# Sparse-graph layer and routed experts on one core: columns of A by way of memory, and by transfers inside the chip

## The chip, the core and the metric

The kernel runs on one core of a Trainium2 chip. Its metric is the device time of one execution in microseconds (us). Three runs of the kernel before gave 504.09, 504.42 and 505.32 us, a median of 504.42. All arithmetic of the parts discussed here is in float32, apart from the one-hot matrices in bf16.

## The reference, cut to what matters

```
x: [2048, 256]; src, dst: 67584 edges, sorted by dst; edge_weight: [67584]
xn  = layernorm(x)
x   = x + segment_sum(edge_weight[:, None] * xn[dst], src, 2048) + node_vec1
xt  = layernorm(x)                              # 2048 tokens of 256
top 2 of 8 experts by softmax(xt @ Wr + br)
x   = x + sum over the two of weight * (gelu(LN(xt) @ W1[e] + b1[e]) @ W2[e] + b2[e])
```

The first part is a sparse 2048 x 2048 matrix A (about 33 entries a column) times xn. The second part is a mixture of experts.

## The kernel before

**Building A densely.** The kernel turns A into dense blocks. A "column block" cb (0 to 15) is the 128 columns of A that meet the 128 rows of xn in block cb; a "half block" n (0 to 31) is 64 of these columns, so cb = n // 2 and h = n % 2 is its half. The loop over n (L463) goes once round for each half block:

- `make_hots(n + 1)` (L299 to L327): VectorE builds the one-hot matrices `hl` (rows within a block, L306) and `eq` (L311) for the next half block and multiplies two thirds of the weights in (L318); GpSimd multiplies the last third (`third`, L325).
- `make_cols(n)` (L329 to L350): TensorE multiplies the one-hots of each group of edges (L343) into the PSUM tile `pa` (3 buffers, two of them used per half block); ScalarE copies each to the SBUF tile `ar` (L346; 3 buffers). In `ar` a partition is a pair of a column and a block of rows, which is not what the later product needs: there a partition must be a column alone. So the rows are turned round by way of memory: SyncE stores `ar` to the DRAM tile `ad` (L347, 512 KB, in rows of 512 bytes), and after the second half reads the whole of it back as the SBUF tile `ac` (L350, 1 MB; partition = column, 8 KB each).
- `dense(cbs, b)` (L352 to L359): TensorE multiplies a group of `ac` tiles with `xn_sb` into the PSUM tile `py1` (2 buffers) for two row blocks b and b + 1, and `add` (L361) puts the result onto `acc` on VectorE, one round later.

**The order.** It is written out by hand: each engine executes its own instructions in the order in which the program names them, SyncE its transfers too. Groups of column blocks are 0-2, 3-5, 6-8, 9-11 and 12-15 (`CS`); each group has 8 calls of `dense`. `todo` holds all 40 calls. From n = 8 on (L500) each round adds 3.5 to a budget, and a call of `dense` costs as much as its group has column blocks (L502 to L504). In the last round (n = 31) all calls of the first four groups that are left are made; the 8 calls of group 12-15 come after the loop (L1077 onward), with the routing and the experts behind them. Between the loop and these stands a branch that all engines take part in (L569).

**Buffers of ac.** Groups take the pools `cols_1` and `cols_0` in turn (`pool_of`, L178), each with 4 buffers. The first tile of a group goes to the one buffer that the group two before it left free; the second tile (blocks 7, 10, 13) goes where that earlier group's first tile was, and so has to wait for the last call of `dense` on that group. The tile `ac` is allocated at h = 1, just ahead of its read (L349).

**After the loop.** SyncE goes on with the weights of the first experts (L932 to L935), the routing runs on VectorE, ScalarE and TensorE, and then TensorE works through the experts' slots (L1013, L1027) until the end.

Of the kernel before, what the change touches and what calls it, by code (L numbers as in the profile page):

```python
# [9 lines left out]
F32 = mybir.dt.float32  # L10
# [11 lines left out]
P = 128  # L22
# [4 lines left out]
def kernel(  # L27
# [30 lines left out]
    nc = tc.nc  # L58
# [3 lines left out]
    NB = N // P  # L62
# [3 lines left out]
    GC = 2  # L66
# [3 lines left out]
    GB = P // GC  # L70
    GH = GB // 2
    QP = P // RK
# [15 lines left out]
    dram = ctx.enter_context(tc.tile_pool(name="dram", bufs=1, space=DRAM))  # L88
# [89 lines left out]
    pool_of = {cb: (cols_1, cols_0)[g % 2] for g, cbs in enumerate(groups) for cb in cbs}  # L178
# [150 lines left out]
    def make_cols(n, hl, hr):  # L329


        cb, h = n // 2, n % 2
        if h == 0:
            ads[cb] = dram.tile([P, NB, P], F32, name="ad", bufs=4)
        ad_v = ads[cb].rearrange("(m j) b r -> (j b) m r", m=GB // QP)
        ar = rowsp.tile([P, GH // QP, P], F32, name="ar")
        for m0 in range(0, GH // QP, 4):
            pa = ps_a.tile([P, 4, P], F32, name="pa")
            for m in range(4):
                for i in range(3):  # L340
                    for j in range(QP):
                        g = (m0 + m) * QP + j
                        nc.tensor.matmul(pa[j * RK:(j + 1) * RK, m, :], hr[:, i, g, :],  # L343
                                         hl[:, g, :], start=(i == 0), stop=(i == 2),
                                         tile_position=(0, j * RK))
            nc.scalar.copy(ar[:, m0:m0 + 4, :], pa)  # L346
        nc.sync.dma_start(ad_v[:, h * GH // QP:(h + 1) * GH // QP, :], ar)  # L347
        if h == 1:
            acs[cb] = pool_of[cb].tile([P, NB, P], F32, name="ac")  # L349
            nc.sync.dma_start(acs[cb], ads[cb])  # L350

    def dense(cbs, b):  # L352

# [14 lines left out]
                                           acc[:, b + i, :D], op0=OP.add, op1=OP.add)  # L368
        nc.vector.tensor_add(acc[:, b:b + 2, D:], acc[:, b:b + 2, D:], pa[:, :, D:DX])

    ads, acs = {}, {}
    ET = mybir.EngineType
    ALL = {ET.DVE, ET.Pool, ET.PE, ET.Activation, ET.SP}
    with tc.manual_schedule(engines=ALL):
# [88 lines left out]
        for n in range(NH):  # L463
# [3 lines left out]
            m = n % 4  # L467
# [26 lines left out]
            for p in late:  # L494
                add(*p)
            late = []
            make_cols(n, *hots.pop(n))


            if n >= 8:  # L500
                budget += 3.5
            while len(todo) > NB // 2 and (budget >= len(todo[0][0]) or n == NH - 1):  # L502
                cbs, b = todo.pop(0)
# [17 lines left out]
            if n == 1:  # L521
# [5 lines left out]
                for rows in (b1_rows, g_rows, be_rows, nv_rows):  # L527
                    m = rows.shape[0]
# [40 lines left out]
    with tc.If(n_used < E):  # L569
# [11 lines left out]
        with tc.tile_pool(name="any", bufs=2) as anyp, tc.tile_pool(  # L581
            name="ps_any", bufs=2, space=PSUM
# [594 lines left out]
    with tc.manual_schedule(engines=ALL - {ET.Pool}):  # L1177
        for q in range(4):
            r = slice(q * N // 4, (q + 1) * N // 4)
# [33 lines left out]
```

## Time and profile before

| What | Value |
|---|---|
| Runs: median (lowest to highest) | 504.42 us (504.09 to 505.32) |
| The profiled execution: its own time | 508.05 us |
| Its span, first to last instruction | 506.3 us, mean granted TensorE clock 0.945 |
| TensorE busy with matmuls | 459.8 us (91%) |
| VectorE, ScalarE, GpSimd busy | 273.1, 183.8, 192.7 us |
| First and last store to `ad` (L347) begun | 31.0 and 192.5 us |
| Read of `ac` (L350): 16, issue to landing | 4.9 to 6.2 us, median 5.9 |
| Store to `ad` (L347): 32, issue to landing | 4.4 to 9.9 us, median 8.7 |
| Dense products of the last group begin (L357) | 209.4 us |

Times inside the execution are counted from the start of the span. A share of busy time is an average: for one stage the busy time of each engine in that stretch is to be read. PE is TensorE, DVE VectorE, ACT ScalarE, POOL GpSimd, SP SyncE; a q behind the name is the engine's queue of transfers, waits and branches. A line such as "ACT ar L346 <- DMA ad<-ar: 5.3, 3, 2.6" says that ScalarE stood 5.3 us in all, 3 times, 2.6 us at the longest, before line 346, until the transfer named had landed.

### The profile page before, as it was taken

What the parts mean: (1) busy time and instruction counts of PE and PEld (TensorE: products, weight loads), DVE (VectorE), ACT (ScalarE), POOL (GpSimd) and SP (SyncE); (2) the same over time, 40 slices, a digit from 0 to 9 for tenths busy, and PEclk for the clock granted to TensorE, in tenths of its full rate; (3) what the DMA queues carried; (4) which work ended last, traced back from release to release, by engine and by line L of the source; (5) the groups of instructions that cost most, each with busy time, mean ns of one, the idle gap of its engine ahead of it and who ended that gap; (6) DMA issues with size and microseconds to landing.
All of it is one profiled execution on the core that took longest, in us unless ns stands there. A gap on an engine that the chain in (4) does not pass through costs nothing.

```text
span 506.3 us, 12113 instructions
## 1 busy us (share of the span) xinstructions
PE 459.8 (91%) x4996; PEld 394.4 (78%) x4996; DVE 273.1 (54%) x621; ACT 183.8 (36%) x422; POOL 192.7 (38%) x158
## 2 busy tenths in 40 slices
PE   4876599898979999899999899999999999999993
PEld 3775478687758878788888788888888888888882
DVE  7999999999969971317837232323232312212111
ACT  2478524144214210028483323332243433333320
POOL 3477655544533330000142444443452444322231
PEclk9575679899979999999999999999999999999998
DMA  6128678796777667953513997997999677226420
GB/s 214 53 76 246 203 223 269 230 236 186 203 216 221 210 178 239 344 189 105 179 54 84 303 333 214 361 356 210 334 360 309 169 210 210 36 40 204 140 92 31
DMA packets 84356, 102.15 MB, mean 202 GB/s; under 512 B 8240, under 2 KB 74656, under 8 KB 82176
## 3 DMA queue, kind: packets, MB, share of 16 engines
q1 hardware_dynamic: 74832, 86.26, 53.5%
q0 software_dynamic: 7984, 13.91, 11.9%
q10 hardware_dynamic: 1472, 1.06, 0.7%
q8 instruction: 44, 0.72, 0.6%
q14 instruction: 24, 0.20, 0.1%
HBM read 75.18 MB, written 28.14 MB: 204 GB/s over the span
## 4 chain that ended last, share of the span: by engine, by line
PE 35%; DMA 13%; issue 3%; DVE 1%; SPq 0%; ACT 0%; POOL 0%; POOLq 0%; DVEq 0%
PE py L1027 16%; PE ph L1013 15%; DMA xs<-xr_d,to_i 8%; DMA y_d<-ys,to_i 2%; DMA out<-y_d 2%; PE px L978 1%; PE px L834 1%; PE py L357 1%; DMA so_far<-out,to_i 1%; DMA out<-ys,to_i 0%; SPq L1180 0%; POOL out L1048 0%; POOLq L1209 0%; ACT L1015 0%; DVE pick L957 0%
## 5 line engine op out<-in xcount | busy, mean ns | idle before, releaser
L357 PE MATMUL py<-xn_sb,ac 128*128 128x264 f32 x512 | 126.3, 404 | 1.8 <-DVEq L569 1.4
L1013 PE MATMUL ph<-xeT,w 128*128 128x256 f32 (+1 forms) x576 | 121.3, 368 | 2.4 <-PEq L1167 1.7
L1027 PE MATMUL py<-w,hT 128*128 128x256 f32 x544 | 121.0, 379 | 0.0
L1013 PEld LDWEIGHTS ph<-xeT,w 128*128 128x128 f32 x576 | 104.4, 190 | 16.5 <-issue 3.0
L357 PEld LDWEIGHTS py<-xn_sb,ac 128*128 128x128 f32 x512 | 98.5, 197 | 21.7 <-issue 2.2
L1027 PEld LDWEIGHTS py<-w,hT 128*128 128x128 f32 x544 | 101.9, 190 | 12.9
L1015 ACT ACTIVATE hT<-ph,ec 128x256 f32<-128x256 f32 (+1 forms) x144 | 66.2, 462 | 117.6 <-PE ph L1013 60.8
L1035 POOL DMA_INDIRECT y_d<-ys,to_i x30 | 48.5, 1616 | 119.3 <-DVE ys L1030 88.5
L318 POOL TENSOR_TENSOR hr<-eq,w 128x1024 bf16<-128x1024 bf16 x32 | 61.2, 1912 | 81.6 <-DVE hr L318 66.1
L343 PE MATMUL pa<-hl,hr 128*32 128x128 bf16 x3072 | 58.4, 237 | 21.6 <-POOL hr L318 10.8
L343 PEld LDWEIGHTS <-hr 128*32 128x32 bf16 x3072 | 50.0, 106 | 32.6 <-issue 14.0
L306 DVE TENSOR_TENSOR hl<-k,iota_t 128x4096 bf16<-128x4096 bf16 x32 | 72.9, 2278 | 0.0
L987 DVE TENSOR_SCALAR xeT<-px,ec 128x256 f32<-128x256 f32 (+1 forms) x38 | 18.4, 526 | 79.8 <-PE px L978 79.0
L939 POOL DMA_INDIRECT xs<-xr_d,to_i x39 | 40.5, 1038 | 54.2 <-DVE z L702 41.9
L346 ACT COPY ar<-pa 128x512 f32<-128x512 f32 x64 | 36.5, 584 | 59.8 <-PE pa L343 53.6
L1030 DVE SCALAR_TENSOR_TENSOR ys<-py,wt,b2w 128x256 f32<-128x256 f32 x34 | 16.4, 484 | 72.7 <-PE py L1027 61.3
L364 DVE TENSOR_TENSOR acc<-acc,py 128x528 f32<-128x528 f32 x32 | 22.3, 701 | 35.3 <-PE py L357 35.3
L318 DVE TENSOR_TENSOR hr<-eq,w 128x2048 bf16<-128x2048 bf16 x32 | 39.1, 1223 | 0.6
L1002 ACT ACTIVATE b2w<-b,wt 128x256 f32<-128x256 f32 x36 | 16.3, 500 | 34.0 <-DVE wt L1000 32.4
L311 DVE TENSOR_TENSOR eq<-k,iota_t 128x1024 bf16<-128x1024 bf16 x32 | 21.8, 680 | 0.0
L670 ACT ACTIVATE sq<-acc,less_m 128x256 f32<-128x256 f32 x16 | 8.0, 499 | 32.6 <-DVE acc L364 32.6
L296 ACT CAST w<-r 128x256 bf16<-128x256 f32 x16 | 6.5, 405 | 25.0 <-DVE r L295 25.0
(196 smaller groups left out, 303.0 us busy)
## 6 DMA issues: line engine op xcount, KB each, us to landing
w<-in_L_ffn_W SPq DMA_DIRECT2D x40, 1024.0 KB, 9.2
ad<-ar SPq DMA_DIRECT2D x32, 512.0 KB, 8.7
ac<-ad SPq DMA_DIRECT2D x16, 1024.0 KB, 5.9
b<-in_L_ffn_b SPq DMA_DIRECT2D x20, 128.0 KB, 9.8
out<-y_d SPq DMA_DIRECT2D x4, 512.0 KB, 6.3
xr_d<-rec SPq DMA_DIRECT2D x1, 1300.0 KB
y_d<-acc SPq DMA_DIRECT2D x1, 1280.0 KB, 5.1
acc<-in_x SPq DMA_DIRECT2D x2, 512.0 KB, 7.6
```

Source lines behind the costliest of these rows:

```text
L306: nc.vector.tensor_tensor(hl.rearrange("p g (n t) -> p g n t", t=2), two(k2[:, 0], g, P), pair(P), OP.is_equal)
L311: nc.vector.tensor_tensor(eq.rearrange("p g (n t) -> p g n t", t=2), two(k2[:, 1], g, RK), pair(RK), OP.is_equal)
L318: return engine.tensor_tensor(hr[:, i0:i1].rearrange("p i g (n t) -> p (i g) n t", t=2), eq[:, None, :, :].to_broadcast([P, i1 - i0, GH, RK]),
L343: nc.tensor.matmul(pa[j * RK:(j + 1) * RK, m, :], hr[:, i, g, :], hl[:, g, :], start=(i == 0), stop=(i == 2), tile_position=(0, j * RK))
L346: nc.scalar.copy(ar[:, m0:m0 + 4, :], pa)
L357: nc.tensor.matmul(pa[:, i, :DX], acs[c][:, b + i, :], xn_sb[:, c, :], start=(c == cbs[0]), stop=(c == cbs[-1]))
L364: nc.vector.tensor_add(acc[:, b:b + 2, :], acc[:, b:b + 2, :], pa[:, :, :DX])
L939: nc.gpsimd.indirect_dma_start(out=(sets[s.set][0] if into is None else into)[:, t, :], out_offset=None, in_=(xr_d if rows is None else ro ...
L1013: nc.tensor.matmul(ph, w1[:, k, c * P:(c + 1) * P], xeT[:, k, :], start=(k == 0), stop=(k == KD - 1))
L1015: nc.scalar.activation(hT[:, c, :s.n * P], ph, AF.Gelu, bias=ec[:, c:c + 1], scale=1.0)
L1027: nc.tensor.matmul(py, hT[:, c, t * P:(t + 1) * P], w2[:, c, :], start=(c == 0), stop=(c == KH - 1))
L1035: st = nc.gpsimd.indirect_dma_start(out=y_d[:, :], out_offset=bass.IndirectOffsetOnAxis(ap=tos[s.to][:, t:t + 1], axis=0), in_=ys, in_offs ...
```

## The change

The rows are turned round without memory: each half block's `ar` goes to `ac` in eight transfers from SBUF to SBUF. Transfer m takes one 128 x 128 slice of `ar` (64 KB: 128 partitions of 512 bytes) to 8 partitions of `ac` (8 KB each). Four are begun after each of the two copies; SyncE begins m = 0 to 4 and ScalarE m = 5 to 7. The tile `ac` is allocated at h = 0, one half block earlier than before. The budget for dense products starts at n = 7, not 8.

```diff
         cb, h = n // 2, n % 2
         if h == 0:
-            ads[cb] = dram.tile([P, NB, P], F32, name="ad", bufs=4)
-        ad_v = ads[cb].rearrange("(m j) b r -> (j b) m r", m=GB // QP)
+            acs[cb] = pool_of[cb].tile([P, NB, P], F32, name="ac")
         ar = rowsp.tile([P, GH // QP, P], F32, name="ar")
         for m0 in range(0, GH // QP, 4):
             pa = ps_a.tile([P, 4, P], F32, name="pa")
...
             nc.scalar.copy(ar[:, m0:m0 + 4, :], pa)
-        nc.sync.dma_start(ad_v[:, h * GH // QP:(h + 1) * GH // QP, :], ar)
-        if h == 1:
-            acs[cb] = pool_of[cb].tile([P, NB, P], F32, name="ac")
-            nc.sync.dma_start(acs[cb], ads[cb])
+            for m in range(m0, m0 + 4):
+
+                c = (h * GH // QP + m) * QP * GC
+                queue = nc.sync if m < 5 else nc.scalar
+                queue.dma_start(acs[cb][c:c + QP * GC], ar[:, m, :])
...
-    ads, acs = {}, {}
+    acs = {}
...
-            if n >= 8:
+            if n >= 7:
                 budget += 3.5
```

Here P = 128, NB = 16, GH = 32, QP = 4, GC = 2, so GH // QP = 8 slices and QP * GC = 8 partitions.

## The prediction

> **What bounds the kernel now.** I read the busy time by stretch first, since the averages of the page mix stages. Columns: length, then busy time of TensorE, its weight loads, VectorE, ScalarE, GpSimd, then granted clock, DMA share, GB/s. The stretches are the loop before and after dense products begin, its tail, and the last group.
>
> ```profile
> 31.00:70.00 39.00, 27.85 (x820) 23.45 (x820) 38.65 (x46) 26.07 (x66) 27.92 (x20) 0.69 0.70 208
> 70.00:190.00 120.00, 111.52 (x2439) 90.58 (x2437) 108.44 (x139) 37.84 (x88) 52.55 (x33) 0.96 0.74 215
> 190.00:209.00 19.00, 17.63 (x160) 14.85 (x160) 4.23 (x6) 1.17 (x2) 0.88 (x4) 1.00 0.84 274
> 209.00:240.00 31.00, 30.43 (x145) 25.85 (x146) 13.55 (x36) 14.23 (x41) 0.00 (x0) 1.00 0.56 188
> ```
>
> To 70 us VectorE is full (38.65 of 39). From 70 to 190 TensorE (111.5 of 120) and VectorE (108.4) are nearly level. Behind 190 TensorE alone sets the end. The DMA engines are three quarters busy throughout.
>
> The waits, second, inside that loop (60 to 192 us; SyncE 30 to 200):
>
> ```profile
> PE pa L343 <- issue: 6.6, 4, 3.1
> PE py L357 <- DMA ac<-ad: 0.4, 1, 0.4
> ACT ar L346 <- DMA ad<-ar: 5.3, 3, 2.6
> DVE acc L364 <- PE py L357: 6.1, 3, 4.2
> SPq L350 <- DMA ad<-ar: 102.9, 19, 9.3
> SPq L350 <- PE py L357: 2.5, 2, 2.3
> ```
>
> SyncE stands 102.9 us for its own stores before it may read back, and stores of later half blocks queue behind. So `ar` comes free late, ScalarE's copy waits 5.3 us, TensorE has holes of 6.6 us and VectorE then waits (4.2 us once). That is all the way through memory costs on the path: about 7 us. The arrival of `ac` itself costs 0.4 us.
>
> Third, the tail in order of time (start, length, what):
>
> ```profile
> 190.42 1.41 PE L343 MATMUL pa<-hl,hr 128*32 128x128 bf16 x88 [1.78 <-POOLq L569]
> 191.76 16.29 PE L357 MATMUL py<-xn_sb,ac 128*128 128x264 f32 x72
> ...
> 198.34 0.33 SPq L350 DMA_DIRECT2D ac<-ad  x1
> ...
> 209.45 0.91 PE L357 MATMUL py<-xn_sb,ac 128*128 128x264 f32 x3 [1.40 <-DVEq L569]
> ```
>
> From 191.76 to 208.0 TensorE works off the dense calls that are left: 72 matmuls, 12 a call, so 6 calls of 2.7 us. Then comes the branch, and at 209.45 the last group. The last `ac` is issued at 198.34 and lands after the median 5.9 us at 204.2, hidden by 5 us.
>
> **The change part by part.**
>
> *Dense products a half block sooner.* Counting the budget (3.5 a round, 3 a call): six rounds make seven calls. From n = 8 the rounds to n = 30 make 26 calls and leave 6; from n = 7 they make 28 and leave 4. The tail loses 2 x 2.7 = 5.4 us. The two calls move forward: one to n = 7, where TensorE has room (27.85 of 39 up to 70 us), one to n = 30, where TensorE now stands 1.8 us for GpSimd at 190.4. Taken at -5.4; were the rounds between full of TensorE work, it would be nearer -2.7.
>
> *What is removed.* 32 stores and 16 reads, with SyncE's 102.9 us of standing. Worth up to the 6.6 us of holes, if the new transfers release `ar` sooner; nothing, if later.
>
> *Issuing.* 256 transfers replace 48. SyncE's 160 at 0.43 us (median issue of L347) are 2.1 us a half block: hidden, for SyncE has nothing else here. ScalarE's 96: its own issues at the start took 0.45 and 0.53 us, so 1.5 us a half block. After 70 us that is 23 x 1.5 = 35 us beside 37.84 busy of 120: hidden. Before 70 us it is 8 x 1.5 = 12 beside 26.07 of 39, nearly full; behind these issues stand ScalarE's next copies of `pa` and the key copies at L281, which VectorE needs three half blocks later (15 us). I take 0; without that cover up to 3 us.
>
> *Waits for a free buffer.* `ac` is written from h = 0. Block 7 starts at n = 14, and its group's eight calls are done in n = 13. Block 10 starts at n = 20, but call 16 is made in n = 20, behind `make_cols`; block 13 starts at n = 26, and call 24 is made in n = 27. SyncE's and now ScalarE's transfers wait there for TensorE, with ScalarE's copies queued behind them, and TensorE waits for those once the third `pa` is full. The row is SyncE's 2.5 us in two waits; for ScalarE one round of 4.3 us for block 13 at most. I take 0 in the sum, as what follows outlasts it.
>
> *The transfers.* No row shows one from SBUF to SBUF, nor one into 8 partitions. Below: the first store alone, in the stretch from 31 to 36 us (packets, MB, share of 16 engines):
>
> ```profile
> q1 hardware_dynamic: 1040, 0.52, 32.7%
> ```
>
> 0.327 x 16 x 5 us / 1040 = 25 ns for a packet of 512 bytes. A half block is still 1024 packets, over 16 engines 1.6 us: the lower end, if the 8 partitions set no limit. Above: the fastest filling of SBUF in the trace, the expert weights into 128 partitions (stretch from 204 to 209.4 us, GB/s in 40 slices):
>
> ```profile
> GB/s 425 425 425 394 394 455 425 425 319 311 349 364 417 372 379 379 387 417 349 372 349 364 357 357 349 349 334 357 349 349 334 288 144 53 83 30 53 64 119 238
> ```
>
> The first eight slices average 421; the share of 8 partitions of 128 is 26.3 GB/s. At that rate a 64 KB transfer takes 2.5 us, and SyncE's five, one after the other with ScalarE's three beside them, 12.5 us a half block: the upper end. The half blocks come every (192.5 - 31.0) / 31 = 5.2 us. I lean to the second row, for it is the one that ends in SBUF; but an issue takes 0.43 us, so the next transfer to other partitions is open long before the first ends, and I reckon two of SyncE's five under way at a time: 6.2 us. That is over 5.2, and so the transfers become the bound: `ar` is held by the half block three back, ScalarE waits for it, `pa` stays full, and TensorE waits.
>
> [...]
>
> *The sum.* First transfer at 31.0, as the first store; 32 x 6.2 = 198.4; the last bytes land some 1.7 us after their data (quickest store 4.4, less 1.6 of data and about 1.1 before it begins). The last `ac` is there at 231.1. TensorE, done with its 4 calls by about 220, starts the last group there instead of at 209.4: +21.7. The -5.4 and the holes lie inside that wait and give nothing. Everything behind hangs on TensorE and shifts along. The span goes from 506.3 to 528; the profiled execution was 508.05 against the median of 504.42, so for the runs I take 504.4 + 21.7 = 526.1.
>
> **The rivals.**
>
> *In time: faster.* If a half block drains in 4.9 us or less (VectorE's own round: 2.28 + 0.68 + 1.23 + 0.70), nothing is late. Then the tail's 5.4 and up to 6.6 of holes are won, less some waits: -2 to -12, about 498. For it: 25 ns a packet and half the bytes moved (512 KB a half block, not 1 MB). Against it: 8 partitions at a time.
>
> *Single file: far slower.* At 8 to 12.5 us a half block the last `ac` lands between 288 and 433: 583 to 728 us. For it: every queue's transfers so far are large and over 128 partitions, so nothing shows small ones overlapping.
>
> *Waits, not data: slower.* The drain holds, but each first use of an `ac` tile waits for 16 landings, not one. At 51 ns for a wait of TensorE's queue (L357 has 9 now), 16 x 15 more are 12 us at most; with 4.3 for block 13 and 3 for ScalarE, less 5.4, up to +14; about 512. It decides once these exceed 5.4 us.
>
> *Gains and losses cancel.* 504.
>
> **How the numbers follow.** Forecast (drain 5.6 to 7.8 us; 507 to 577) 0.42; in time 0.35; single file 0.12; waits 0.06; cancel 0.05. Slower is 0.42 + 0.12 + 0.06 = 0.60. A change under 0.3% (1.5 us) can't be told from none. The range runs from 495, into the fast case, to 577; it leaves out single file and the fast case's best. The likeliest case's own range is 507 to 577.
>
> **What would show it.** Right: DMA engines busy but the transfers landing later and later after issue, ScalarE's L346 waiting tens of us for `ac<-ar`, TensorE with holes from 70 to 190, the last group beginning near 230. Wrong: landings steady under 10 us, L346 not waiting for them, four dense calls in the tail, the last group beginning near 200. [...] The whole forecast hangs on one unshown price; at 5.5 us a half block (31.0 + 32 x 5.5 + 1.7 = 208.7) nothing is lost, and below it the sign turns.

## The result, and the profile after

The change makes the kernel slower: 549.05 us in the median of four runs (540.75, 545.32, 552.78 and 562.29) against 504.25 us. The ratio of 1.0765 (95% interval 1.0683 to 1.0847) leaves out the two runs of the changed kernel that lie over 1.5% above its fastest, and makes the loss 38.6 us. The forecast was 526 us within 495 to 577, a loss of 21.7 us. The profiled execution took 545.32 us with a span of 543.6 us, 37.3 us more than before.

The same stretches as before, with the same columns (length, busy time of TensorE, its weight loads, VectorE, ScalarE, GpSimd, then clock, DMA share, GB/s), of the changed kernel:

```profile
31.00:70.00 39.00, 26.83 (x692) 24.80 (x694) 30.96 (x39) 21.17 (x53) 21.91 (x16) 0.91 0.64 101
70.00:190.00 120.00, 102.74 (x2140) 83.06 (x2133) 99.28 (x130) 37.53 (x94) 50.76 (x33) 0.92 0.56 103
190.00:209.00 19.00, 13.93 (x324) 10.99 (x323) 12.99 (x13) 2.15 (x4) 6.13 (x4) 0.93 0.46 71
209.00:240.00 31.00, 24.30 (x284) 19.55 (x282) 10.02 (x15) 3.22 (x6) 2.43 (x4) 0.99 0.60 77
```

No engine is full any more. VectorE, which had almost no gap up to 70 us, is busy 7.7 us less there (38.65 to 30.96) and 9 us less up to 190 (108.44 to 99.28). The stretch from 209 to 240, once TensorE's last group, now holds rounds of the loop. The GB/s have halved (208 to 101 and 215 to 103 in the first two stretches), since nothing goes to memory and back; the DMA engines' busy share has fallen far less (0.74 to 0.56 between 70 and 190 us). That is the first sign that a packet takes longer.

Who waited for whom in the changed kernel from 30 to 260 us (us in all, times, longest), picked from the waits of TensorE, ScalarE, VectorE and SyncE:

```profile
PE pa L342 <- ACT ar L345: 22.7, 8, 6.9
PE py L357 <- DMA ec<-cols_d: 7.7, 1, 7.7
PE py L357 <- DMA ac<-ar: 5.9, 2, 4.5
...
ACT ar L345 <- DMA ac<-ar: 61.6, 13, 8.5
...
ACT w L296 <- DMA ac<-ar: 19.4, 8, 3.4
...
DVE r L295 <- ACT w L296: 14.3, 3, 6.1
DVE used_i L557 <- PE pa L556: 9.0, 1, 9.0
...
SPq L350 <- DMA ac<-ar: 82.4, 77, 7.0
```

Read from below: SyncE stands 82.4 us, at 77 of its 160 transfers, until an earlier transfer has landed. (By the trace's semaphore records the 256 transfers report their landing on eight semaphores, and each waits until the transfer that used its semaphore before has landed: the first report of a semaphore behind an issue comes 1.03 us after it at the soonest. So at most eight are under way.) So the transfers are begun late, `ar` comes free late, and ScalarE's copy waits 61.6 us where it waited 5.3. TensorE then waits for the copy (22.7 us), and VectorE for ScalarE and TensorE.

The tail of the loop in order of time:

```profile
204.54 34.98 SPq L350 DMA_DIRECT2D ac<-ar  x27
...
221.25 10.95 PE L357 MATMUL py<-xn_sb,ac 128*128 128x264 f32 x48
...
233.61 1.61 PE L357 MATMUL py<-xn_sb,ac 128*128 128x264 f32 x6 [1.41 <-DMA ac<-ar]
...
242.92 19.31 PE L357 MATMUL py<-xn_sb,ac 128*128 128x264 f32 x76 [7.70 <-DMA ec<-cols_d]
```

The tail has 48 matmuls, 4 calls, as counted. TensorE ends them at 232, tries the last group at 233.6 and stands 7.7 us more for its last block. The releaser named there, the load of `ec`, is not what it waits for: SyncE is still beginning transfers of `ac` until 239.5. The last group runs from 242.9, not 209.45. So 33.5 of the 37.3 us are lost before it. The other 3.8 lie behind; the granted clock was 0.83 there from 240 to 260 us, against 1.00 before from 209 to 240, but how much of the 3.8 us that makes was not separated.

### The profile page after: what moved, and what is told of

Same layout as the page of the kernel before. It is cut to its first block, busy times and chain, and to the rows that moved or that the text cites. A ratio compares the mean times of both kernels' runs of the same rounds, so it can differ in the third digit from the quotient of the medians.

```text
span 543.6 us, 12497 instructions
## 1 busy us (share of the span) xinstructions
PE 474.0 (87%) x4996; PEld 406.1 (75%) x4996; DVE 273.7 (50%) x621; ACT 182.7 (34%) x422; POOL 192.5 (35%) x158
## 4 chain that ended last, share of the span: by engine, by line
PE 36%; DMA 12%; issue 3%; DVE 1%; ACT 1%; SPq 0%; POOL 0%; POOLq 0%; DVEq 0%; ACTq 0%
PE py L1027 15%; PE ph L1013 14%; DMA xs<-xr_d,to_i 8%; PE py L357 4%; DMA y_d<-ys,to_i 2%; DMA out<-y_d 1%; PE px L978 1%; PE px L834 1%; DMA so_far<-out,to_i 1%; DMA out<-ys,to_i 0%; SPq L1180 0%; DMA ec<-cols_d 0%; POOL out L1048 0%; DVE acc L364 0%; ACT L1015 0%
## 5 line engine op out<-in xcount | busy, mean ns | idle before, releaser
L357 PE MATMUL py<-xn_sb,ac 128*128 128x264 f32 x512 | 130.7, 412 | 14.2 <-DMA ec<-cols_d 7.7
L357 PEld LDWEIGHTS py<-xn_sb,ac 128*128 128x128 f32 x512 | 99.8, 201 | 37.0 <-issue 17.2
L1027 PEld LDWEIGHTS py<-w,hT 128*128 128x128 f32 x544 | 102.8, 192 | 13.3
L342 PE MATMUL pa<-hl,hr 128*32 128x128 bf16 x3072 | 62.5, 246 | 33.0 <-ACT ar L345 22.7
L342 PEld LDWEIGHTS <-hr 128*32 128x32 bf16 x3072 | 55.1, 111 | 43.4 <-issue 35.6
L345 ACT COPY ar<-pa 128x512 f32<-128x512 f32 x64 | 34.8, 584 | 76.5 <-DMA ac<-ar 61.6
L410 PEld LDWEIGHTS pa<-wc,ar 128*128 128x128 f32 x64 | 14.0, 332 | 3.5 <-ACT ar L404 3.3
```

The lines of the kernel that those rows point to most:

```text
L357: nc.tensor.matmul(pa[:, i, :DX], acs[c][:, b + i, :], xn_sb[:, c, :], start=(c == cbs[0]), stop=(c == cbs[-1]))
L1027: nc.tensor.matmul(py, hT[:, c, t * P:(t + 1) * P], w2[:, c, :], start=(c == 0), stop=(c == KH - 1))
```

## The experiments

Where an experiment leaves A scrambled, the routing and the slots behind it differ, so the start of the last group's products is compared, not the whole time. These kernels and the one with SyncE alone ran once each, and the changed kernel's four runs lie up to 21.5 us apart, so differences of a few us between them are not read as effects. The shortest of the four took 4.6 us less than the profiled one, so a gap of some 20 us to the changed kernel's 242.9 stands.

The profile's sum of packet times gives the mean time of a packet: share x 16 engines x stretch / packets, all over 30 to 200 us (170 us). This counts every packet of the two queues, and a tenth to a seventh of them are not the 512-byte packets of these transfers but mostly packets of 4 and 48 bytes. It is a measure for comparing. The 512-byte packets alone, over all 256 transfers of a trace, come in the same order and are given below.

**Where the transfers go.** Three kernels change the destination alone.

```diff
-                queue.dma_start(acs[cb][c:c + QP * GC], ar[:, m, :])
+# d128
+                queue.dma_start(acs[cb][:, h * 8 + m, :], ar[:, m, :])
+# d8_step4
+                queue.dma_start(acs[cb][32 * ((m + 8 * h) // 4) + m % 4:32 * ((m + 8 * h) // 4 + 1):4], ar[:, m, :])
+# d16
+                queue.dma_start(acs[cb][16 * m:16 * m + 16, 8 * h:8 * h + 8, :], ar[:, m, :])
```

> The changed kernel, but each 64 KB transfer goes to all 128 partitions of ac (512 bytes in each) instead of to 8 partitions (8 KB in each). Same 256 transfers, same packets, queues and buffers; the elements of A land in other places, so A is scrambled, the routing and the number of experts' slots behind it change, and only the start of the last group's dense products (L357 behind the branch; 209.4 us before, 242.9 us with the change) is to be read. Theory P (the few partitions written limit a transfer): a half block drains in about 2 to 4 us, ScalarE no longer waits for ac<-ar, last group at 196 to 206. Theory E (the transfer runs on too few DMA engines): the same. Theory W (256 transfers, each waiting for the landing of earlier ones in its queue, whatever their data): last group at 235 to 245 as now.

> The changed kernel, but each transfer goes to 8 partitions four apart (0, 4, .. 28 of a quarter) instead of 8 neighbours. A is scrambled, so the start of the last group alone is to be read (209.4 before, 242.9 with the change). Theory P: neighbours share a way in and partitions four apart don't, so a half block drains in under 5 us, last group at 198 to 210. Theory E (8 partitions keep a transfer to half the engines, whichever they are): 235 to 245 as now, or if the engines' own packet time of 25 ns holds, 3.2 us a half block and under 210; then the packets in the trace would still run on half the engines. Theory W: 235 to 245.

> The changed kernel, but each transfer goes to 16 neighbouring partitions (4 KB in each) instead of 8. A is scrambled, so the start of the last group alone is to be read (209.4 before, 242.9 with the change). Theory P: twice the partitions take twice the rate, SyncE's five need about 3 us a half block, last group at 198 to 210. Theory E: about the same gain. Theory W: 235 to 245 as now.

Measured: the last group begins at 204.90 (all 128 partitions), 208.23 (8 partitions four apart) and 207.35 (16 neighbours). The DMA queues from 30 to 200 us (packets, MB, share of 16 engines), first of the changed kernel:

```profile
q1 hardware_dynamic: 19128, 9.04, 30.8%
q10 hardware_dynamic: 10974, 5.29, 18.5%
```

of the kernel with 128 partitions:

```profile
q1 hardware_dynamic: 24873, 11.51, 23.5%
q10 hardware_dynamic: 13824, 6.30, 12.8%
```

and of the one with partitions four apart:

```profile
q1 hardware_dynamic: 22120, 10.48, 22.6%
q10 hardware_dynamic: 13056, 6.29, 13.6%
```

Adding the two queues, a packet takes 0.493 x 16 x 170 / 30102 = 44.5 ns with the change, 25.5 ns over 128 partitions and 28.0 ns four apart; 16 neighbours lie between at 36.4. The 512-byte packets alone take 50.1, 27.2, 29.4 and 39.4 ns. From its issue to its landing, by the semaphore records, a transfer takes 4.5 us in the median with the change (9.6 at most), 2.2 over 128 partitions, 2.7 four apart and 3.5 with 16 neighbours. Number, size, queues and buffers of the transfers are the same in all four. So theory W, the mere number of transfers, is out. Theory E is out too: 8 partitions four apart are as few as 8 neighbours and cost almost nothing. What costs is that the 8 partitions are neighbours: 50.1 ns a packet against 29.4 four apart. The starts lie in theory P's three ranges; that neighbours share a way in, as it has it for the second kernel, was the author's assumption, and no run shows why they are slower. Even over all 128 partitions the last group begins only 4.5 us before the 209.45 of the kernel before, and four apart 1.2 us: in single runs, too little to call a gain from leaving memory.

**Which queue begins them.** All by SyncE:

```diff
-                queue = nc.sync if m < 5 else nc.scalar
+                queue = nc.sync
```

> The changed kernel, but SyncE begins all eight transfers of a half block. Theory P, with one queue's transfers going in single file at the 1.3 us each that the tail of the changed kernel shows for SyncE alone (27 in 35 us): 8 x 1.3 = 10.4 us a half block, last ac at 31 + 333 + 2 = 366, last group near 365, time near 670. Theory E (the engines' work sets the rate, whichever queue): no change, last group near 243, time 540 to 560. Theory S (ScalarE, blocked by transfers in its queue, is what costs): faster than the change, last group near 215.

Measured: 519.0 us (one run, beside 507.55 for the kernel before), last group at 219.53 (six of its products already at 213.28). Of the direct versions that leave A in place it is the fastest. What SyncE did in this kernel, and then who waited there from 30 to 245 us (TensorE, ScalarE, SyncE):

```profile
L350 SPq DMA_DIRECT2D ac<-ar x256: 604/613/1799, 30.0 to 216.1; - x128
```

```profile
PE py L357 <- DMA ac<-ar: 11.5, 3, 5.3
...
PE pa L342 <- ACT ar L345: 6.0, 6, 2.4
...
ACT ar L345 <- DMA ac<-ar: 57.4, 17, 5.9
...
SPq L350 <- DMA ac<-ar: 2.8, 9, 0.6
```

256 transfers are begun in 186 us, 0.73 us each, of which 0.61 is the issue itself; SyncE stands only 2.8 us for landings. Packets take 0.481 x 16 x 170 / 32825 = 39.9 ns, longer than spread ones (the 512-byte packets alone 41.9), and a transfer lands 3.6 us after its issue in the median: at this pace, in time. ScalarE's copy still waits 57.4 us in all, nearly as long as with the change, but TensorE waits for that copy only 6.0 us instead of 22.7. So the sum of ScalarE's waiting is not what the time goes by. Theory P as it was put, single file at 1.3 us, is out: one queue alone carries 64 KB every 0.73 us into 8 neighbours. The 1.3 us in the tail of the changed kernel were not the time of a transfer but stands between transfers: of the 35 us of that row 16.6 are standing for landings, and 27 issues at 0.61 us are as much again. Theory S fits this run, so the next ones go against it.

**Both at once.**

> Both edits at once: destinations of 8 partitions four apart, and all eight transfers begun by SyncE. A is scrambled, so the start of the last group alone is to be read; with the three runs there are it makes a table of two by two (neighbours, two queues 242.9; neighbours, SyncE alone 219.5; four apart, two queues 208.2). Theory Q (the second queue costs because ScalarE stands in it, whatever the data): about 23 us better than with two queues here too, as far as the issue allows: 32 x 8 x 0.61 = 157 us, so 200 to 204. Theory C (the second queue costs because transfers to neighbours collide and land late, and ScalarE stands for these): with destinations that don't collide one queue or two is the same, 205 to 211.

Measured: six products of the last group from 208.03, the rest from 214.46. The table of two by two, start of the last group (where it begins twice, the second):

| | SyncE and ScalarE | SyncE alone |
|---|---|---|
| 8 neighbours | 242.9 | 219.5 |
| 8 partitions four apart | 208.2 | 214.5 |

With spread destinations two queues are 6 us ahead; SyncE alone takes 5.7 us a half block to begin its transfers there (30.0 to 211.9 us for 256, 0.71 each, of which 0.61 is the issue). With neighbours the second queue costs 23 us. Theory Q, that ScalarE standing in its queue costs whatever the data, is out: it wanted 200 to 204. Theory C's range of 205 to 211 holds for the first six products alone; its account fits the table, once SyncE's issuing is added.

**Whose transfers go to neighbours.** With the destinations of one queue alone spread over the same partitions:

```diff
+                at = acs[cb][c:c + QP * GC]
+# act_apart
+                if m >= 5:
+                    at = acs[cb][64 * h + 40 + m - 5:64 * h + 64:3]
+# sp_apart
+                if m < 5:
+                    at = acs[cb][64 * h + m:64 * h + 40:5]
-                queue.dma_start(acs[cb][c:c + QP * GC], ar[:, m, :])
+                queue.dma_start(at, ar[:, m, :])
```

> The changed kernel, with SyncE's five transfers to 8 neighbours as they are and ScalarE's three to 8 partitions three apart in the same 24 partitions. A is scrambled, so the start of the last group alone is to be read (242.9 with the change, 208.2 with all transfers spread, 219.5 with SyncE alone and neighbours). Theory S (the harm is that ScalarE, an engine with other work, stands for transfers that land late): ScalarE's own land early now, it stands little, 210 to 222. Theory D (the harm is transfers of both queues under way together, whoever stands): five of eight still collide, 225 to 238.

> The mirror: SyncE's five transfers go to 8 partitions five apart in the same 40 partitions, ScalarE's three to 8 neighbours as they are. A is scrambled, so the start of the last group alone is to be read. Theory S: ScalarE still stands for late landings, 225 to 240. Theory D: only three of eight collide, 210 to 222. If both runs lie near 210 to 222, only the number of colliding transfers under way matters, and not who begins them.

Measured: the last group begins at 222.06 (with a stand, again at 224.68) with ScalarE's spread, and at 219.58 with SyncE's spread; packets take 41.3 and 37.9 ns, SyncE stands 60.5 and 52.2 us for landings. The second run speaks against theory S, for ScalarE's own transfers still go to neighbours there; the first lies on the edge between the two. Spreading either part gives 18 to 23 of the 35 us that spreading all gives. So it matters more how many of the transfers go to neighbours than which queue begins them. A share of the loss that comes from ScalarE's standing is not excluded by these two runs.

**Which transfers share a moment.** Two splits of four and four (m even and odd; m below 4 and above):

```diff
-                queue = nc.sync if m < 5 else nc.scalar
+# d8_even_odd
+                queue = nc.sync if m % 2 == 0 else nc.scalar
+# d8_low_high
+                queue = nc.sync if m < 4 else nc.scalar
```

> The changed kernel with its transfers to 8 neighbours, but SyncE begins m = 0, 2, 4, 6 and ScalarE m = 1, 3, 5, 7. Transfers m and m + 4 fill partitions 32 apart; here both are always in the same queue. Theory K (what collides is the two queues' transfers to partitions 32 apart): packets as with SyncE alone (37 to 47 ns in the mean against 36 to 69 with the change), last group at 206 to 218, time 503 to 516. Rival L (packets collide inside each transfer, and a second queue only doubles their number): 225 to 245, as with the other split of four and four. Rival M (ScalarE standing in its queue costs, and it has four transfers now, not three): over 243.

> The changed kernel, but SyncE begins m = 0 to 3 and ScalarE m = 4 to 7, so that the two queues' transfers under way at a time fill partitions 32 apart (0 and 4, 1 and 5, and so on). Theory K: the worst split, last group at 243 to 265, time 545 to 565. Rival L: like the split into even and odd. Rival M: like the split into even and odd, over 243.

Measured: 560.29 us (ratio 1.109, 1.0998 to 1.1181), last group at 255.99; and 565.55, 568.80, 583.37 and 583.88 us, last group at 264.3 and again at 267.85. Theory K fails: keeping transfers to partitions 32 apart in one queue does not cure it. The second split is the slower, as K had it, but the bulk is in both: packets of 55.5 and 57.4 ns. Rival L's 225 to 245 is missed by both. Rival M's number is met by both. The table above has shown that ScalarE's part costs nothing where the destinations are spread (208.2 with it, 214.5 without); where they are neighbours, it was not separated, and in the second split ScalarE's cast at L296 waits 69.9 us for transfers (19.4 with the change). The mean landing time over the time between two issues gives an estimate of the transfers under way: 5.5 with SyncE alone, 6.1 with the change, 7.0 and 7.4 with the even splits, of at most eight. The packets get longer in the same order. Late landings raise that estimate themselves, so it goes with the account but doesn't prove it. Which transfers meet at which moment was not resolved, nor was it tried whether two queues would do better with more than eight semaphores.

**The other part alone, and the way through memory with less standing.** The budget from n = 7 in the kernel before:

> One part of the change alone: the way through memory stays, the budget starts at n = 7. Theory of the forecast: two calls leave the tail (6 to 4, 5.4 us less there), but at n = 7 TensorE stands until the ac of block 2 has landed (68.9 us in the profile before, about 6 us after it would start), and later rounds are full of TensorE work; last group at 205 to 209, time 500 to 504. Rival: the start is worth its whole 5.4 us, last group at 204, time 499. Other rival: the stand at n = 7 makes VectorE late and nothing is left, 504 to 507.

And SyncE's read put behind the store of the next half block, with the budget from n = 8 and n = 7:

```diff
-        if h == 1:
-            acs[cb] = pool_of[cb].tile([P, NB, P], F32, name="ac")
-            nc.sync.dma_start(acs[cb], ads[cb])
+        if h == 0 and cb > 0:
+            read_back(cb - 1)
+
+    def read_back(cb):
+
+        acs[cb] = pool_of[cb].tile([P, NB, P], F32, name="ac")
+        nc.sync.dma_start(acs[cb], ads[cb])
...
             make_cols(n, *hots.pop(n))
+            if n == NH - 1:
+                read_back(NB - 1)
```

> The kernel before with one edit: SyncE begins the read of a column block only after the store of the next half block, so that it doesn't stand in front of its queue until the last store has landed (102.9 us in all before). Budget from n = 8. Theory: stores no longer queue behind that wait, ar comes free in time, TensorE's holes of 6.6 us close and VectorE doesn't wait for them; last group at 203 to 207, time 498 to 502. Rival: TensorE is full anyway and the holes move elsewhere: 207 to 210, 503 to 506.

> The same with the budget from n = 7. If both add up: last group at 199 to 204, time 494 to 499. If TensorE's work between 70 and 190 us is the limit, the same as the better of the two alone, 498 to 503.

Measured in ten runs each, beside 505.25 us for the kernel before: 506.87 us for n = 7 alone (ratio 1.0062, 1.0028 to 1.0096), 501.65 us for the later read (0.9935, 0.9887 to 0.9983), 507.99 us for both (1.005, 1.0012 to 1.0088). All three are small. The tail with n = 7 alone, and then two waits from 60 to 192 us:

```profile
197.91 10.95 PE L357 MATMUL py<-xn_sb,ac 128*128 128x264 f32 x48 [2.28 <-issue]
210.26 25.16 PE L357 MATMUL py<-xn_sb,ac 128*128 128x264 f32 x112 [1.40 <-DVEq L569]
```

```profile
PE py L357 <- DMA ac<-ad: 4.8, 1, 4.8
...
DVE acc L367 <- PE py L357: 8.3, 1, 8.3
```

The tail has lost its two calls, and yet the last group begins 0.8 us later than before: the last round starts its calls at 197.9 instead of 191.8. At n = 7 TensorE stood 4.8 us for the first `ac`, and VectorE then stood 8.3 us for those products. VectorE had no such time to give: up to 70 us it was busy for 38.65 of 39 us before and for 34.59 here. That is the second rival of this run, and its range of 504 to 507 us holds. Of the later read, the tail, and then SyncE's standing in front of a read (now L354):

```profile
189.67 16.29 PE L361 MATMUL py<-xn_sb,ac 128*128 128x264 f32 x72
207.35 8.03 PE L361 MATMUL py<-xn_sb,ac 128*128 128x264 f32 x35 [1.40 <-DVEq L575]
```

```profile
SPq L354 <- DMA ad<-ar: 19.3, 7, 6.0
```

SyncE stands 19.3 us instead of 102.9, and the last group begins 2.1 us sooner. The time lies in the theory's range, the last group's start in the rival's. TensorE's waits between 60 and 192 us have not become fewer (12.2 us before, 13.3 here): they have moved. The granted clock was 0.99 from 70 to 190 us, against 0.96 before, so what gave the 2.1 us is not settled. Of the versions that leave A in place this one alone is ahead of the kernel before, by 0.65%. The two edits do not add up: with n = 7 the last group begins at 211.54, and both ranges given for it are missed.

## Why the prediction was right, and where its steps were not

*The bound moves to the transfers, and ScalarE waits for `ar`.* Shown: 61.6 us of waiting at L345, TensorE with 22.7 us of waits for ScalarE's copy, last group at 242.9 where the sum had 231.1. From 30.0 to 239.5 the transfers took 6.5 us a half block; the sum had 6.2. The span came out 15.6 us over the sum's 528: 11.8 up to the last group, 3.8 behind it. One sign did not come as described: no transfer took more than 9.6 us from issue to landing, which was to speak against the forecast. As a late landing puts off the issue of a later transfer, the lateness shows in SyncE's standing. Two rivals fall by the same profile: a half block took 6.5 us, not the 4.9 or less of "in time", and TensorE's queue has 66 waits at L357 instead of 9, not the 240 more of "waits, not data".

*Why they take 6.2 us.* This is the step that failed; that its size came out near is luck. It took 8 partitions to be slow to fill as such, and two of SyncE's five to be under way at a time at 2.5 us each. The runs show no such rate: SyncE alone sends 64 KB every 0.73 us into groups of 8 neighbours, each landing after 3.6 us in the median, so that about five are under way (an estimate, 3.6 over 0.73); and 8 partitions four apart cost little more than 128 (29.4 ns a packet against 27.2). What makes the half block long is that transfers to neighbours of both queues, under way together, take 44.5 ns a packet in the mean (25 to 28 spread, 39.9 with SyncE alone, 55 to 57 with four from each queue) and land late (4.5 us after the issue in the median, 9.6 at most), and that both queues then stand for landings (SyncE's 82.4 us). By that reasoning one queue alone should have been slower, and its last group began 23 us sooner.

*The rival of single file* (583 to 728 us) falls with it: with SyncE alone the time was 519.0. There the transfers followed each other at 0.73 us, each to other partitions than the last, and landed 3.6 us after their issue in the median, so they overlapped. The second queue moved the start of the last group in both directions, 6 us sooner with partitions four apart (214.5 to 208.2) and 23 us later with neighbours (219.5 to 242.9).

*Issuing.* Mis-sized: 0.61 us on SyncE and 0.62 on ScalarE, not 0.43 and 0.5, as the row of the changed kernel shows (shortest, median and longest in ns):

```profile
L350 SPq DMA_DIRECT2D ac<-ar x160: 604/614/1597, 30.0 to 238.9; - x160
L350 ACTq DMA_DIRECT2D ac<-ar x96: 623/624/1261, 31.3 to 229.6; - x96
```

SyncE's 160 make 98 us; with 82.4 of standing that is 180 of the 210 us that the transfers span. The kernel with 128 partitions has 0.59 and 0.61 us there, so the few partitions are not what makes the issue long. ScalarE's three make 1.9 us a half block, and they stand ahead of the work that VectorE needs:

```profile
160.09 1.07 ACT L345 COPY ar<-pa 128x512 f32<-128x512 f32 x2 [3.26 <-DMA ac<-ar]
161.80 1.95 ACTq L350 DMA_DIRECT2D ac<-ar  x3
163.79 0.40 ACT L296 CAST w<-r 128x256 bf16<-128x256 f32 x1 [2.62 <-DMA ac<-ar]
```

Here the copies end at 161.16, the three issues run from 161.80 to 163.75, and only then comes the cast at L296. Most of the 2.62 us that it is said to wait for a transfer is issuing, which the profile doesn't count as busy. VectorE waited 14.3 us for that cast in all. With partitions four apart the cast is held up for nearly as long (18.2 us), and VectorE waits 3.4 us for it: the issuing alone costs little. The prediction named the key copies at L281 as what queues behind ScalarE's transfers, and took 0 to 3 us; it missed the cast, for which VectorE waits in the same round.

*Dense products sooner.* The count was right (6 calls to 4), its worth of 5.4 us was not: alone it costs 0.6%. The forecast had allowed for rounds full of TensorE work, but only down to a gain of 2.7 us, and not for VectorE, which was the full engine at n = 7. In the sum the term counted for nothing.

*What is removed.* The 6.6 us of holes were taken as the most that leaving memory could give. The later read takes away most of SyncE's standing and the last group begins 2.1 us sooner, with TensorE's waits no shorter in sum. So the 6.6 us were not simply there to be won.

## What to carry to other kernels

When one large transfer is cut into many small ones, cost the issue of each from a row of its own shape (0.61 us here for 64 KB from SBUF to SBUF, not the 0.43 of the 512 KB store), and list what stands behind it on the engine that begins it, down to the shortest slack. Look at which partitions a transfer fills, and at how many such transfers are under way at once: with 8 neighbouring partitions, a transfer landed 3.6 us after its issue in the median when one queue began them all here, and 4.5 us when two did. Before moving work out of a tail, look whether the rounds that take it have time to spare on every engine that handles its result; here VectorE had none (38.65 us busy of 39 up to 70 us), and it gained nothing (506.87 us against 505.25).

## What the runs showed that was not expected

- One transfer of 64 KB to 8 neighbouring partitions every 0.73 us is sustained from one queue (256 in 186 us, 2.8 us of standing), while the same transfers from two queues took longer in all: 242.9 us against 219.5 to the last group, and 256.0 with an even split.
- Beginning a transfer of 64 KB from SBUF to SBUF took SyncE 0.61 us in the median where the destination had 8 partitions and 0.59 us where it had 128, against 0.43 us for the 512 KB store.
- The mean packet of the queues that carry the SBUF-to-SBUF transfers ranged from 25.5 ns (128 partitions) over 28.0 (8, four apart) and 36.4 (16 neighbours) to 57.4 ns (8 neighbours, four transfers from each queue); the 512-byte packets alone from 27.2 over 29.4 and 39.4 to 62.3 ns.
- The landing of a 64 KB transfer, in the median, ranged from 2.2 us after its issue (128 partitions) to 6.4 us (the same split of four and four).
